# Two of the seven single tiles of the routed experts stand in a block that runs only if the routing has more than 37 groups

## The chip, the cores and the metric

The kernel runs on one core of a Trainium2 chip. The metric is the device time of one execution in microseconds (us); the time before is the median of three runs.

## What is computed

A decoder layer on 2048 rows (8 sequences of 256) of width 256, all in float32: causal self-attention with 16 heads, then three rounds of attention against a context with a gated recurrent update, then a feed-forward layer with one shared expert and eight routed ones, a layer norm after each. The change is in the routed experts:

```python
router_probs = softmax(x @ gate_w + gate_b)                    # 2048 x 8
expert_values, expert_indices = top_k(router_probs, k=2)
expert_values = expert_values / (sum(expert_values) + 1e-9)
h = gelu(einsum('bsd,edi->bsei', x, ew1) + eb1)                # 256 -> 1024, for each expert
all_outputs = einsum('bsei,eid->bsed', h, ew2) + eb2           # 1024 -> 256
moe_out = sum over the two chosen experts of value * output
x = layernorm(x + mlp(x, sh_w1, sh_b1, sh_w2, sh_b2) + moe_out)
```

Each row goes to two of eight experts, so 4096 rows are to be worked, and how many each expert gets is known only when the kernel runs.

## The kernel before

The rows are worked expert by expert, and the kernel is unrolled: the number of pieces is fixed when it is written. A group is 128 rows of one expert. A pair tile is two groups (256 rows), a single tile is one. 16 pair tiles (numbers 0 to 15, `NPAIRT`) and 7 single tiles (16 to 22, `NSINGLE`) cover any routing, since eight experts can have at most 39 groups. What a tile works on is looked up.

`place` computes for each row the line of a table `xd` in memory where its copy goes, and POOL scatters the rows there, block by block. `tables()` then counts on VectorE how many pairs and singles each expert has, and gives each tile its expert (`te`, as an integer `tei`) and the first line of its rows (`tr`, `tri`). A tile with no owner takes lines that hold zeros and the last expert, and is worked like any other. `left_no` says which left-over group a tile may take: the singles take 0 to 6, the last pair tile may take group 7.

For each tile, SP reads expert and line into registers and issues the loads: `tile_fetch` the rows `xg` (four buffers), `tile_weights` the first weight w1 (1 MB) and its bias, `tile_weights2` the second, w2 (1 MB), and its bias (two buffers each). `tile_turn` transposes the rows on TensorE, `tile_up` multiplies with w1 into PSUM `ph_t` (two buffers) and ScalarE applies the gelu into `hT_t`, `tile_down` multiplies with w2 into `pf_t`, VectorE adds the bias into `yo`, and SP stores `yo` into the table `yd`.

The order is written by hand. `TILES` lists two pairs and a single seven times, and the two last pairs behind them. The loop's turn k does the up product of tile k, issues the row fetch of k + 3 and w1 of k + 2, turns k + 1, does the down product of k - 1, and issues w2 of k + 1. The shared expert works on eight units of 256 rows (`shared_up`, `shared_down`: `ph_s`, `pf_s`): four before the tile loop, while rows are scattered and tables made, and four behind it.

Behind the loop a fixed order begins for PE, ACT, DVE and POOL (`manual_schedule`). There POOL gathers the results back from `yd`, 32 gathers of 128 rows (`fetch_back`, 16 buffers `y`), DVE weighs and adds them (`take_back`), and `finish` norms the rows and stores them, while PE works the shared units 4 to 7. The first lines of it:

```python
    shared_up(4)
    fetch_back(0)
    shared_up(5)
    fetch_back(1)
    take_back(0)
    parts(4)
    take_back(1)
```

A gather may read any line of `yd`, so it comes behind all stores of the loop.

Of the kernel before, what the change touches and what calls it, by code (L numbers as in the profile page):

```python
# [10 lines left out]
F32 = mybir.dt.float32  # L11
I32 = mybir.dt.int32
U16 = mybir.dt.uint16
AF = mybir.ActivationFunctionType
ALU = mybir.AluOpType
# [6 lines left out]
NE, FF = 8, 1024  # L22
# [11 lines left out]

RT = 256
NSTEP = NT // RT
NPAIRT = 2 * NT // RT
NSINGLE = (2 * NT + NE * (P - 1)) // P - 2 * NPAIRT  # L40
NTILE = NPAIRT + NSINGLE

TILES = [t for k in range(NSINGLE) for t in (2 * k, 2 * k + 1, NPAIRT + k)]
TILES += range(2 * NSINGLE, NPAIRT)

ROWS = NE * NT + RT

# [14 lines left out]
def decoder_kernel(  # L62
# [538 lines left out]
        count(pair_no, slice(NPAIRT + h, NTILE, 2), [[1, n]], NPAIRT)  # L601
    count(pair_row, one, [[P, NSINGLE]], NPAIRT * RT)
    nc.gpsimd.memset(left_no[:, two], float(NT))
    nc.gpsimd.memset(left_no[:, NPAIRT - 1 : NPAIRT], float(NSINGLE))
    count(left_no, one, [[1, NSINGLE]])

    gate_b = fr.tile([P, NE], F32, name="gate_b")
# [4 lines left out]
    def tt(o, a, b, op):  # L612
        nc.vector.tensor_tensor(o, a, b, op)  # L613
# [306 lines left out]
    def tables():  # L920

        pt = bank("total")[:, 0:NE]
        nc.tensor.matmul(pt, ones, before[:, nsub_all, :], start=True, stop=True)
        total = fr.tile([P, NE], F32, name="total")
        nc.vector.tensor_copy(total, pt)
        none = float(NE * NT)

        def steps_below(name, x):

            more = fr.tile([P, NE, NSTEP], F32, name=f"more_{name}")  # L930
            shape = [P, NE, NSTEP]
            tt(more, x.unsqueeze(2).to_broadcast(shape), steps_rt.unsqueeze(1).to_broadcast(shape), ALU.is_gt)
            num = fr.tile([P, NE], F32, name=f"num_{name}")
            nc.vector.tensor_reduce(num, more, AX.X, ALU.add)
            return num

        def ends(name, num):

            end = [fr.tile([P, NE], F32, name=f"end_{name}{k}") for k in range(2)]
            nc.vector.tensor_copy(end[0], num)  # L940
            q, step = 0, 1
            while step < NE:
                nc.vector.tensor_copy(end[1 - q][:, 0:step], end[q][:, 0:step])
                tt(end[1 - q][:, step:], end[q][:, step:], end[q][:, : NE - step], ALU.add)
                q, step = 1 - q, 2 * step
            return end[q]

        def owners(name, end, no):

            shape = [P, NTILE, NE]  # L950
            past = fr.tile(shape, F32, name=f"past_{name}")
            tt(past, end.unsqueeze(1).to_broadcast(shape), no.unsqueeze(2).to_broadcast(shape), ALU.is_le)
            te = fr.tile([P, NTILE], F32, name=f"te_{name}")
            nc.vector.tensor_reduce(te, past, AX.X, ALU.add)
            return te

        def looked_up(name, te, origin):
            shape = [P, NTILE, NE + 1]
            mine = fr.tile(shape, F32, name=f"mine_{name}")
            tt(mine, te.unsqueeze(2).to_broadcast(shape), experts.unsqueeze(1).to_broadcast(shape), ALU.is_equal)  # L960
            tt(mine, mine, origin.unsqueeze(1).to_broadcast(shape), ALU.mult)
            tr = fr.tile([P, NTILE], F32, name=f"tr_{name}")
            nc.vector.tensor_reduce(tr, mine, AX.X, ALU.add)
            return tr

        anyof = steps_below("any", total)
        nc.vector.tensor_scalar(total, total, -float(P), None, ALU.add)
        pairs = steps_below("pairs", total)  # L970
        left = fr.tile([P, NE], F32, name="left")
        tt(left, anyof, pairs, ALU.subtract)
        pair_end, left_end = ends("pairs", pairs), ends("left", left)

        pair_origin = fr.tile([P, NE + 1], F32, name="pair_origin")
        left_origin = fr.tile([P, NE + 1], F32, name="left_origin")
        for origin in (pair_origin, left_origin):
            nc.vector.tensor_copy(origin, first_row)
        nc.vector.scalar_tensor_tensor(
            left_origin[:, 0:NE], pairs, float(RT), first_row[:, 0:NE], ALU.mult, ALU.add  # L980
        )
        tt(pairs, pair_end, pairs, ALU.subtract)
        nc.vector.scalar_tensor_tensor(
            pair_origin[:, 0:NE], pairs, -float(RT), first_row[:, 0:NE], ALU.mult, ALU.add
        )
        te = owners("pairs", pair_end, pair_no)
        tr = looked_up("pairs", te, pair_origin)
        tt(tr, tr, pair_row, ALU.add)
        nc.vector.tensor_scalar(tr, tr, none, None, ALU.min)

        over = fr.tile([P, 1], F32, name="over")
        nc.vector.tensor_scalar(over, pair_end[:, NE - 1 : NE], -float(NPAIRT), 0.0, ALU.add, ALU.max)
        nc.vector.tensor_scalar(over, over, -2.0, None, ALU.mult)
        tt(left_no[:, one], left_no[:, one], over.to_broadcast([P, NSINGLE]), ALU.add)
        te2 = owners("left", left_end, left_no)
        tr2 = looked_up("left", te2, left_origin)
        free = fr.tile([P, NTILE], F32, name="free")
        nc.vector.tensor_scalar(free, te, float(NE), None, ALU.is_ge)
        for a, b, n in ((te, te2, float(NE)), (tr, tr2, none)):
            nc.vector.scalar_tensor_tensor(b, b, -n, free, ALU.add, ALU.mult)  # L1000
            tt(a, a, b, ALU.add)
        nc.vector.tensor_scalar(te, te, float(NE - 1), None, ALU.min)
        tei = fr.tile([P, NTILE], I32, name="tei")
        nc.vector.tensor_copy(tei, te)
        tri = fr.tile([P, NTILE], I32, name="tri")
        nc.vector.tensor_copy(tri, tr)
        return tei, tri
# [120 lines left out]
    def tile_fetch(t):  # L1128

        row = nc.sync.value_load(tri[0:1, t : t + 1], min_val=0, max_val=ROWS - RT)  # L1130
        xg = f2.tile([P, 2, D], F32, tag="xg", name=f"xg_{t}", bufs=4)[:, 0 : groups(t), :]
        load = nc.sync.dma_start(xg, rows_of(xd, row, t))
        for put in puts:
            tc.add_manual_dep(
                load.ins,
                put.ins.name,
                mybir.DependencyInfo(mybir.DependencyClass.Sync, mybir.DependencyReason.DATA),
                reason="rows of the table",
            )
        TI[t] = [row, xg]  # L1140

    def tile_weights(t):

        e = nc.sync.value_load(tei[0:1, t : t + 1], min_val=0, max_val=NE - 1)
        w1_sb = wff.tile([P, DC, FF], F32, tag="w1", name=f"w1_{t}")
        w2_sb = wff.tile([P, FC, D], F32, tag="w2", name=f"w2_{t}")
        bt = f2.tile([P, FC], F32, tag="bt", name=f"bt_{t}", bufs=3)
        b2t = f2.tile([P, D], F32, tag="b2t", name=f"b2t_{t}", bufs=3)
        nc.sync.dma_start(w1_sb, ew1[ds(e, 1), :, :].rearrange("e (c p) f -> p (e c) f", p=P))
        nc.sync.dma_start(bt, vecs[:, ds(e * FC, FC)])  # L1150
        TI[t] += [w1_sb, w2_sb, bt, b2t, e]

    def tile_weights2(t):

        row, xgT, w1_sb, w2_sb, bt, b2t, e = TI[t]
        nc.sync.dma_start(w2_sb, ew2[ds(e, 1), :, :].rearrange("e (c p) d -> p (e c) d", p=P))
        nc.sync.dma_start(b2t, b2[ds(e, 1), :].to_broadcast([P, D]))
# [12 lines left out]
    def tile_up(t):  # L1170
        row, xgT, w1_sb, w2_sb, bt, b2t, e = TI[t]
        HT["t", t] = up(w1_sb, bt, xgT, f"t{t}")

    def tile_down(t):
        row, xgT, w1_sb, w2_sb, bt, b2t, e = TI.pop(t)
        n = groups(t)
        po = down(w2_sb, HT.pop(("t", t)), f"t{t}", groups=n)
        yo = f2.tile([P, 2, D], F32, tag="yo", name=f"yo_{t}")[:, 0:n, :]
        tt(yo, po[:, 0:n, :], b2t.unsqueeze(1).to_broadcast([P, n, D]), ALU.add)
        nc.sync.dma_start(rows_of(yd, row, t), yo)  # L1180
# [68 lines left out]
    for k, t in enumerate(TILES):  # L1249
        tile_up(t)  # L1250
        for t2 in TILES[k + 3 : k + 4]:
            tile_fetch(t2)
        for t2 in TILES[k + 2 : k + 3]:
            tile_weights(t2)
        for t2 in TILES[k + 1 : k + 2]:
            tile_turn(t2)
        if k:
            tile_down(TILES[k - 1])
        for t2 in TILES[k + 1 : k + 2]:
            tile_weights2(t2)  # L1260


    tile_down(TILES[-1])
    engines = {mybir.EngineType.PE, mybir.EngineType.Activation, mybir.EngineType.DVE, mybir.EngineType.Pool}
    ctx.enter_context(tc.manual_schedule(engines=engines))
    half = NSUB // 2
# [95 lines left out]
```

## Time and profile before

| what | value |
|---|---|
| time, median of 3 runs | 1041.12 us (1041.05 to 1042.68) |
| the profiled execution's own time | 1039.3 us |
| its span, first to last instruction | 1037.6 us |
| mean granted TensorE clock | 0.999 |
| tile loop, from its first up product to the last down product on PE | 695.2 to 975.7 us |
| shared units 4 to 7 on PE behind it | 975.6 to 1031.0 us |

The profile is one execution. Engines are PE (TensorE matmul), PEld (its weight loads), DVE (VectorE), ACT (ScalarE), POOL (GpSimd) and SP, which issues the DMAs. Names such as `ph_t<-xgT,w` are out<-in by the program's tiles, L1062 is a line of the kernel. One float32 matmul of the program appears as two records, so a single tile's up product of 16 is 32 in a row. In a timeline, brackets give how long the engine was idle before, and what ended it; for a wait on several things the name can be that of one long done. Several helpers (`tt`, the norms) have one line for all their uses, so the tile's name is read with it.

### The profile page before, as it was taken

The page shows a single profiled execution, that of the slowest core. Times are in us where ns is not written, and L with a number is a line of the kernel's source. Part 1 is how long each engine was busy: PE and PEld are TensorE (multiplying, and loading weights), DVE is VectorE, ACT ScalarE, POOL GpSimd, SP SyncE. Part 2 cuts the span into 40 slices and gives each one's busy share as a digit, 9 for nine tenths or more (in the row PEclk, how much of TensorE's full clock was granted, in tenths as well). Part 3 has the DMA queues.
Part 4 walks back from the last instruction along what each step waited for, and adds up shares of the span by engine and source line. Part 5 has one row for each costly group of instructions (what it writes and reads, how often), then busy time and mean ns, then how long its engine had stood idle before and what let it go on. Part 6 is the DMA issues. An engine that isn't in the chain of part 4 may idle for free. (4 is left out here: it accounts for less than half of the span.)

```text
span 1037.6 us, 13707 instructions
## 1 busy us (share of the span) xinstructions
PE 1023.9 (99%) x4686; PEld 711.2 (69%) x4686; DVE 486.6 (47%) x1378; ACT 466.3 (45%) x1156; POOL 264.1 (25%) x280
## 2 busy tenths in 40 slices
PE   9999999999999999999999999999999999999997
PEld 5444555555546755556565567988888888888886
DVE  4778776877897542444444579600010101010157
ACT  3568776766685034455455434322222322222232
POOL 2333422633587221122212014410000000000172
PEclk9999999999999999999999999999999999999999
DMA  9844434434467399950000001166666676765143
GB/s 324 132 76 93 86 69 76 77 62 76 77 115 161 125 348 348 349 172 0 1 1 0 1 16 57 62 193 228 219 219 213 224 235 221 230 208 194 50 121 103
DMA packets 195492, 144.24 MB, mean 139 GB/s; under 512 B 107551, under 2 KB 185951, under 8 KB 195423
## 3 DMA queue, kind: packets, MB, share of 16 engines
q1 hardware_dynamic: 191263, 132.88, 45.5%
q0 software_dynamic: 3072, 8.39, 2.5%
q10 hardware_dynamic: 1088, 2.10, 0.5%
q8 instruction: 37, 0.61, 0.2%
q14 instruction: 32, 0.26, 0.1%
HBM read 72.70 MB, written 45.48 MB: 114 GB/s over the span
## 5 line engine op out<-in xcount | busy, mean ns | idle before, releaser
L1071 ACT ACTIVATE hT_t<-ph_t,bt 128x256 f32<-128x256 f32 (+1 forms) x184 | 71.3, 438 | 202.6 <-issue 139.1
L353 ACT ACTIVATE sc<-sc,nmax 128x128 f32<-128x128 f32 (+1 forms) x256 | 113.2, 443 | 86.0 <-DVE nmax L340 85.5
L368 POOL TENSOR_TENSOR sc<-sc,sums 128x256 f32<-128x256 f32 (+1 forms) x128 | 105.4, 845 | 162.8 <-DVE sums L365 162.0
L1062 PE MATMUL ph_t<-xgT,w 128*128 128x256 f32 (+1 forms) x736 | 140.3, 348 | 0.8 <-ACT hT_t L1071 0.8
L1076 PE MATMUL pf_t<-w,hT_t 128*128 128x256 f32 x624 | 138.3, 379 | 0.0
L1062 PEld LDWEIGHTS ph_t<-xgT,w 128*128 128x128 f32 x736 | 123.8, 190 | 15.0 <-ACT hT_t L1071 1.0
L756 PE MATMUL gate<-XT,whh_sb 128*128 128x512 f32 x288 | 133.8, 593 | 0.0
L1076 PEld LDWEIGHTS pf_t<-w,hT_t 128*128 128x128 f32 x624 | 116.9, 190 | 15.0
L1190 POOL DMA_INDIRECT y<-yd,slot x32 | 31.0, 969 | 308.2 <-PE ph_s L1062 298.7
L396 DVE COPY pT<-turned 128x1536 uint16<-128x1536 uint16 x64 | 89.8, 1403 | 1.2 <-DMA turned<-planes 1.2
L756 PEld LDWEIGHTS gate<-XT,whh_sb 128*128 128x128 f32 x288 | 54.2, 189 | 48.5 <-issue 46.2
L340 DVE CUSTOM_DVE_ANT_0 sc<-pp,mask 128x128 f32<-128x128 f32 (+1 forms) x256 | 75.8, 352 | 8.8 <-PE pp L328 8.2
L1167 DVE COPY xgT<-xg 128x512 f32<-128x512 f32 (+1 forms) x23 | 14.0, 610 | 131.7 <-PE xg L1165 131.7
L765 PEld LDWEIGHTS gate<-at,G 120*128 120x128 f32 x288 | 54.5, 189 | 29.9 <-issue 23.3
L613 DVE TENSOR_TENSOR yo<-pf_t,b2t 128x512 f32<-128x512 f32 (+1 forms) x23 | 14.0, 610 | 127.9 <-PE pf_t L1076 127.9
L384 ACT COPY planes<-sc 128x1536 uint16<-128x1536 uint16 x48 | 70.6, 1470 | 6.7 <-POOL sc L368 6.7
L765 PE MATMUL gate<-at,G 120*128 120x256 f32 x288 | 72.1, 379 | 0.4 <-DVE at L613 0.4
L303 PE MATMUL pq<-XT,wq_sb 128*128 128x512 f32 x128 | 63.4, 618 | 0.2 <-DVE XT L105 0.2
L303 PE MATMUL pq<-XT,wk_sb 128*128 128x512 f32 x128 | 63.2, 616 | 0.0
L313 PE MATMUL pv<-wv_sb,XT 128*128 128x512 f32 x128 | 59.7, 594 | 0.0
L410 PE MATMUL po<-pT,v 128*64 128x256 f32 (+1 forms) x512 | 55.7, 338 | 2.4 <-DVE pT L396 1.5
L426 PE MATMUL py<-wo_sb,ot 128*128 128x256 f32 x256 | 57.9, 381 | 0.0
(209 smaller groups left out, 1429.5 us busy)
## 6 DMA issues: line engine op xcount, KB each, us to landing
w<-in_ew_dram SPq DMA_DIRECT2D x46, 1024.0 KB, 5.5
xd<-zeros SPq DMA_DIRECT2D x1, 16640.0 KB, 51.3
yd<-zeros SPq DMA_DIRECT2D x1, 16640.0 KB, 99.4
xg<-xd SPq DMA_DIRECT2D x16, 256.0 KB, 5.2
yd<-yo SPq DMA_DIRECT2D x16, 256.0 KB, 5.6
b2t<-in_b_dram SPq DMA_DIRECT2D x23, 128.0 KB, 5.3
sh<-in_sh_w_dram SPq DMA_DIRECT2D x2, 1024.0 KB, 6.6
X<-in_x_dram SPq DMA_DIRECT2D x3, 512.0 KB, 11.6
```

The source lines that it names most:

```text
L303: nc.tensor.matmul(pq, w[:, dc, ts(pr, P)], XT[i][:, dc, :], start=dc == 0, stop=dc == DC - 1)
L313: nc.tensor.matmul(pv, XT[i][:, dc, ts(n, P)], wv_sb[:, dc, ts(hf, 512)], start=dc == 0, stop=dc == DC - 1)
L340: nc.vector.tensor_tensor_reduce(out=sc[:, h, seg[t]], in0=pp[h][:, seg[t]], in1=mask[:, seg[t]], scale=-(HD**-0.5), scalar=3.0e38, op0=AL ...
L353: nc.scalar.activation(sc[:, h, seg[t]], sc[:, h, seg[t]], AF.Exp, scale=-1.0, bias=nmax[:, t, h : h + 1], accum_out=sums[:, t, h : h + 1],)
L368: nc.gpsimd.tensor_tensor(sc[:, :, seg[t]], sc[:, :, seg[t]], sums[:, t, :].unsqueeze(2).to_broadcast([P, 2, w]), ALU.mult,)
L384: nc.scalar.copy(planes, words)
L396: nc.vector.tensor_copy(pT.rearrange("p h c -> p (h c)").bitcast(U16).rearrange("p (n w) -> p w n", w=2), turned.rearrange("p (w c) q -> p ...
L756: nc.tensor.matmul(pg[:, oc, :], whh_sb[:, dc, o], XT[i][:, dc, :], start=dc == 0, stop=not given and dc == DC - 1,)
L765: nc.tensor.matmul(pg[:, oc, ts(bi, S)], G[:, BPB * i + bi, o], AT_[p][:, bi, :], start=not hidden, stop=not hidden or bi == BPB - 1,)
L1062: nc.tensor.matmul(ph[:, a, 0:w], w1_sb[:, dc, ts(c, P)], rhs[:, dc, :], start=dc == 0, stop=dc == DC - 1,)
L1071: nc.scalar.activation(hT[:, c, 0:w], ph[:, a, 0:w], AF.Gelu_apprx_tanh, bias=bias[:, c : c + 1])
L1076: nc.tensor.matmul(po, hT[:, c, ts(a, P)], w2_sb[:, c, :], start=c == 0, stop=c == FC - 1)
```

## The change

Five single tiles (`NOFTEN`) stay in `TILES`. The two last (`RARE`, tiles 21 and 22) stand behind the loop in `with tc.If(first_rare < NE)`, each written out as fetch, weights, turn, up and down. The tables hand left-over groups to the five singles first, then to pair tiles that have no pair, then to the rare ones: `spare`, the number of free pair tiles, is added to the rare tiles' `left_no`, and three pair tiles instead of one may take a left-over group. One more integer in `tei` holds tile 21's expert before it is limited to 7; it is 8 (`NE`) where that tile has no owner. It is read into a register of every engine in turn k = 16 of the loop.

```diff
+NRARE = 2
+NOFTEN = NSINGLE - NRARE
-TILES = [t for k in range(NSINGLE) for t in (2 * k, 2 * k + 1, NPAIRT + k)]
-TILES += range(2 * NSINGLE, NPAIRT)
+TILES = [t for k in range(NOFTEN) for t in (2 * k, 2 * k + 1, NPAIRT + k)]
+TILES += range(2 * NOFTEN, NPAIRT)
+RARE = range(NTILE - NRARE, NTILE)
...
-    nc.gpsimd.memset(left_no[:, NPAIRT - 1 : NPAIRT], float(NSINGLE))
+    for j in range(NE - NOFTEN):
+        nc.gpsimd.memset(left_no[:, NPAIRT - 1 - j : NPAIRT - j], float(NOFTEN + j))
...
+        spare = fr.tile([P, 1], F32, name="spare")
+        nc.vector.tensor_scalar(spare, pair_end[:, NE - 1 : NE], -1.0, float(NPAIRT), ALU.mult, ALU.add)
+        nc.vector.tensor_scalar(spare, spare, 0.0, None, ALU.max)
+        rare = slice(RARE.start, NTILE)
+        tt(left_no[:, rare], left_no[:, rare], spare.to_broadcast([P, NRARE]), ALU.add)
...
+        tei = fr.tile([P, NTILE + 1], I32, name="tei")
+        nc.vector.tensor_copy(tei[:, NTILE : NTILE + 1], te[:, RARE.start : RARE.start + 1])
         nc.vector.tensor_scalar(te, te, float(NE - 1), None, ALU.min)
-        tei = fr.tile([P, NTILE], I32, name="tei")
-        nc.vector.tensor_copy(tei, te)
+        nc.vector.tensor_copy(tei[:, 0:NTILE], te)
...
         if k:
             tile_down(TILES[k - 1])
+        if k == NPAIRT:
+            first_rare = nc.values_load(tei[0:1, NTILE : NTILE + 1], min_val=0, max_val=NE)
         for t2 in TILES[k + 1 : k + 2]:
             tile_weights2(t2)


     tile_down(TILES[-1])
+    with tc.If(first_rare < NE):
+        for t in RARE:
+            tile_fetch(t)
+            tile_weights(t)
+            tile_weights2(t)
+            tile_turn(t)
+            tile_up(t)
+            tile_down(t)
```

## The prediction

> **What bounds the kernel now.** I read the page first, then the busy time of the engines by stage, then the chain of waits in order of time, then the timeline around the spot where the new block stands, and last single rows for the costs. The page and the stage row say that TensorE is full:
>
> ```profile
> PE 1023.9 (99%) x4686; PEld 711.2 (69%) x4686; DVE 486.6 (47%) x1378; ACT 466.3 (45%) x1156; POOL 264.1 (25%) x280
> PEclk9999999999999999999999999999999999999999
> ...
> 703.00:976.00 273.00, 272.43 (x1400) 242.79 (x1401) 26.70 (x45) 68.11 (x177) 0.00 (x0) 1.00 0.63 210
> ```
>
> In the third line (from 703 us, when the tile loop has just begun, to its end at 976) PE is busy for 272.43 of 273.00 us at clock 1.00, with the DMA engines at 0.63. So time taken off PE there is time taken off the end, as long as PE stays fed. The chain of waits (start, length, what) confirms it; the lines of one single tile and the end of the loop:
>
> ```profile
> 890.14 0.22 PE xg L1165 x2
> ...
> 897.27 3.71 PE ph_t L1062 x32
> ...
> 915.67 3.46 PE pf_t L1076 x16
> ...
> 961.92 13.81 PE pf_t L1076 x64
> 975.73 13.81 PE ph_s L1062 x64
> ...
> 1010.26 6.92 PE ph_s L1062 x32
> ...
> 1017.21 0.84 ACT hT_s L1071 x2
> ```
>
> The chain is PE without a break from 703.57 to 1017.19, then ACT and DVE for the last norms. A single tile stands in it three times: 2 matmuls that turn its rows (0.22), 32 of the up product (3.71), 16 of the down product (3.46).
>
> **Is the block skipped?** Everything rests on this. The reference, evaluated with its own inputs, sends 540, 521, 707, 391, 600, 463, 533 and 341 rows to the eight experts. In groups of 128 that is 5+5+6+4+5+4+5+3 = 37, in the kernel's terms 16 pairs and 5 singles. The condition needs more than 37. The nearest step to 38 is expert 7 (43 rows short of 384) or expert 4 (40 short of 640), so rounding can't reach it. With 16 pairs nothing is spare, single 5 finds no owner in either table, its expert number is 8 = NE, and `first_rare < NE` is false. Tiles 21 and 22 carry no row today either.
>
> **What is removed.** Two single tiles: 2 x (0.22 + 3.71 + 3.46) = 14.78 us of PE, all in the chain. Their 4.2 MB of weights, 16 activations, 4 vector operations and stores go too; these lie beside PE and bring nothing. The loop now ends in six pairs instead of two. A pair takes 0.44 + 6.91 + 6.91 = 14.26 us and loads about 2.4 MB with its rows and bias, 170 GB/s, under the 210 GB/s that this stage moves today, so I charge nothing; w2 is issued a whole tile ahead of its use, while
>
> ```profile
> w<-in_ew_dram SPq DMA_DIRECT2D x46, 1024.0 KB, 5.5
> ```
>
> says 5.5 us from issue to landing.
>
> **What is added to the tables.** Two scalar operations for `spare`, one add onto `left_no`, one more cast. Rows:
>
> ```profile
> L992 DVE TENSOR_SCALAR over<-end_pairs x1: 136/136/136, 670.7 to 670.7; 128x1 f32<-128x1 f32 x1
> ...
> L613 DVE TENSOR_TENSOR left_no<-left_no,over x1: 157/157/157, 671.4 to 671.4; 128x7 f32<-128x7 f32 x1
> ...
> L1004 DVE CAST tei<-te_pairs x1: 177/177/177, 674.4 to 674.4; 128x23 int32<-128x23 f32 x1
> ...
> 682.48 1.64 SPq L1132 DMA_DIRECT2D xg<-xd  x2
> ```
>
> 2 x 0.14 + 0.16 + 0.18 = 0.62 us, so `tri` is ready at 675.3 instead of 674.7. The first row fetch starts only at 682.48, because it waits for the scatters into `xd` that POOL issues until 680.8. The 0.6 us vanish in those 7 us; without that cover they would be 0.6 us. Two more POOL memsets (0.09 us each, at 330 us) lie where POOL is mostly idle: nothing.
>
> **What is added to the queues.** `values_load` puts one register load on each of five engines. SP's row is the price:
>
> ```profile
> L1130 SPq TENSOR_LOAD <-tri x23: 262/267/600, 674.8 to 723.7; - x23
> ```
>
> 0.27 us. On PE it stands ahead of `tile_weights2` in the loop's turn k = 16, long after its data; the matmuls already queued hide it, at worst 0.27 us. Behind it on ACT and DVE only work with slack is queued, POOL is idle for 299 us there, and on SP it is ahead of a w2 load with a tile of slack.
>
> **The block's edge, the unknown.** No instruction of before branches in mid-kernel, and the trace doesn't show how the semaphores that the skipped instructions would have raised are settled. What lies around it:
>
> ```profile
> 975.77 0.69 DVE L613 TENSOR_TENSOR yo<-pf_t,b2t 128x512 f32<-128x512 f32 x1 [6.22 <-PE pf_t L1076]
> ...
> 979.47 0.98 POOL L1190 DMA_INDIRECT y<-yd,slot  x1 [298.71 <-PE ph_s L1062]
> ...
> 1012.11 0.84 ACT L1071 ACTIVATE hT_s<-ph_s,vec_sb 128x256 f32<-128x256 f32 x2
> ...
> L1358 SPq DRAIN  x3: 7/13/130, 1036.7 to 1037.3; - x3
> ...
> L1358 PEldq EVENT_SEMAPHORE  x2: 51/51/51, 1036.9 to 1037.6; - x2
> ```
>
> Today PE runs from `pf_t` into `ph_s` without a gap, and under those shared matmuls the last `yo` is written, stored, and gathered back (gather 3.9 us after PE's tail began). The bounds: from below 0.3 us (a register test and a branch; a gain is excluded, as PE has no gap to close). From above, PE waits for everything that the arm could touch, the last store into `yd` among it: it stands until the first gather could start, 3.9 us. The nearest row is the end of the program, where all engines meet: drains and semaphore passes from 1036.7 to 1037.6, 0.9 us a meeting. One to enter and one to leave make 1.8 us, with nothing of it hidden since PE has no work on the other side of the edge. I take 1.8 and keep 0.3 and 3.9 as ends. The gather may also come later than 3.9 us after the tail's start, since POOL must pass the edge too. Its slack is small: take-back of block 1 waited for gathers at 1001.76, the norms behind it hold ACT until the 1012.11 row, and PE would have missed that buffer at about 1013.5, 0.5 us after ACT freed it at 1012.95. In the case taken PE is late by as much as POOL, so nothing is added.
>
> Two rules of the Trainium skill speak against the change. "TensorE: Matmul & The Clock Gate" (Part 1, the HAM clock gate) says that PE falls to half clock after an idle window of about 3.4 us and needs another 3.4 us of work to come back. The row above has PEclk 9 in every slice, and PE's longest stop in the tile stage is 0.83 us, so no run shows it here. With my 1.8 us nothing follows; with the upper end of 3.9 us the rule adds an estimated 3.4 / 2 = 1.7, making 5.6. "Runtime: NRT & Kernel Launch" (Instruction fetch mechanics) says that a taken branch to a target outside the resident pages stalls until the page is fetched. The row:
>
> ```profile
> q8 instruction: 37, 0.61, 0.2%
> ```
>
> 37 packets of 0.61 MB in all, 16.5 KB each; if q8 is PE's, 9,372 instructions make 253 per packet. The skipped arm has 2 x 50 matmuls and as many weight loads on PE, 200, less than one packet. So the next page should hold the target: 0 in my sum. By the rule's other case it would be one transfer, 2.1 us (the fastest store into `yd`) to 5.5 (a weight load).
>
> **Sum.** On the profiled execution: span 1037.6 - 14.78 + 1.8 = 1024.6. That execution took 1039.3 in all, 1.8 less than the median 1041.12; carried over, 1041.1 - 14.8 + 1.8 = 1028.1.
>
> **Rivals.**
> *The edge waits for the store.* For it: the arm writes `yd` and reuses the `yo` buffers, so what guards the arm may wait for that store. Against: PE's own part of the arm touches neither. Cost 3.9 to 5.6 us, in all 1030.2 to 1032.0; with the table or gather a little late, 1032.5.
> *Code is fetched after the branch.* For it: five instruction streams jump at once, and SP's or ACT's may sit near a page's end. Against: PE's arm is short. 1.8 to 5.6 plus 2.1 to 5.5: 1030.2 to 1037.4.
> *Slower: the block runs.* If the switch is true for this routing (a slip in the tables or in the order of clip and copy), both tiles run alone at the edge: nothing prefetched, so PE stands for about 7.9 us (median landing of the first weights), and the 4.2 MB at about 230 GB/s last until 18 us; then the second down product 3.5, `yo` 0.4, the store and restart 3.9: 26 us in place of 14.8, and 1.8 for the edges. 1041.1 + 13 = 1054. It decides when the eighth expert number is below 8; by my count it is 8. The same sign needs over 14.8 us of edge otherwise, nearly four whole store waits in a row.
>
> **How the numbers follow.** Forecast 0.55 (1026.6 to 1029.5, from the edge's 0.3 to 3); store wait 0.25; code fetch 0.10; block runs 0.03; an edge dearer than all of this 0.05, of which half ends near today's time; more gain than 14.8 us 0.02. The range 1026.0 to 1034.5 holds the first two and most of the third. A difference below 0.2% (2.1 us, about the spread of the runs before) can't be told from none. Faster 0.91, same 0.03, slower 0.06.
>
> **What would show it.** Right: PE's count of `pf_t` falls by 32, to 592, and of `ph_t` by 64, to 672; the last `pf_t` ends near 961; a hole on PE of 1 to 3 us stands before `ph_s`; first gather 3 to 5 us behind the last `pf_t`. A hole near 4 us with a clock below 1 behind it means the store rival; a hole longer than that, with instruction packets in it, the code rival; 736 matmuls of `ph_t` mean that the block ran. I am wrong if PE shows new gaps inside the loop, or if the tail from `ph_s` to the end grows.

## The result, and the profile after

The changed kernel takes 1026.46 us (median of 4 runs, 1024.52 to 1028.01) against 1041.9 (1041.05 to 1042.8): ratio 0.9857, 95% interval 0.9843 to 0.9872, so 13 to 16 us less. The profiled execution took 1024.52 us with a span of 1022.8, where that of before took 1039.3 with 1037.6. A second set of runs gave 0.9851 (0.983 to 0.987).

The page of the changed kernel, with the busy row of the engines, the clock row and the two groups of the tile loop on PE:

```profile
PE 1009.1 (99%) x4586; PEld 697.2 (68%) x4586; DVE 485.0 (47%) x1378; ACT 461.0 (45%) x1140; POOL 263.6 (26%) x282
...
PEclk9999999999999999999999999999999999999999
...
L1075 PE MATMUL ph_t<-xgT,w 128*128 128x256 f32 (+1 forms) x672 | 132.5, 355 | 0.8 <-ACT hT_t L1084 0.8
...
L1089 PE MATMUL pf_t<-w,hT_t 128*128 128x256 f32 x592 | 131.1, 379 | 0.0
```

PE has 100 matmuls fewer, two single tiles of 50 each: 64 of `ph_t` (736 before), 32 of `pf_t` (624), 4 that turn rows. PE's busy time fell by 14.8 us and the span by 14.8. PEclk reads 9 in every slice, as before.

The timeline of the changed kernel at the spot of the block (start, length, engine, line; in brackets the idle time before):

```profile
946.89 13.98 PE L1089 MATMUL pf_t<-w,hT_t 128*128 128x256 f32 x64
...
954.72 7.30 SPq L1193 DMA_DIRECT2D yd<-yo  x2
960.91 0.69 DVE L618 TENSOR_TENSOR yo<-pf_t,b2t 128x512 f32<-128x512 f32 x1 [6.21 <-PE pf_t L1089]
960.99 13.68 PEld L1075 LDWEIGHTS ph_s<-XT,sh 128*128 128x128 f32 x64 [0.52 <-issue]
961.02 14.05 PE L1075 MATMUL ph_s<-XT,sh 128*128 128x256 f32 x64
963.08 0.84 ACT L1084 ACTIVATE hT_s<-ph_s,vec_sb 128x256 f32<-128x256 f32 x2 [15.15 <-PE ph_s L1075]
964.58 0.98 POOL L1203 DMA_INDIRECT y<-yd,slot  x1 [283.93 <-ACT hT_s L1084]
```

The same spot in the kernel before:

```profile
961.75 13.98 PE L1076 MATMUL pf_t<-w,hT_t 128*128 128x256 f32 x64
...
975.57 13.98 PE L1062 MATMUL ph_s<-XT,sh 128*128 128x256 f32 x64
```

There the `pf_t` row ends at 961.75 + 13.98 = 975.73 and the next begins at 975.57: in a stream without a gap the next row begins 0.16 us before the end of the one ahead of it. In the changed kernel the last `pf_t` row ends at 946.89 + 13.98 = 960.87, so the next would begin at 960.71. It begins at 961.02, and PE lost 961.02 - 960.71 = 0.31 us at the block's edge. I call this the hole. The first gather comes 3.87 us behind 960.71; before it was 3.9 behind 975.57.

The accounts of the two traces close. The tile loop begins at 695.13 instead of 695.23. From there to `ph_s` it takes 265.89 us instead of 280.34, which is 14.45 less: 14.78 of two tiles and the hole back. From `ph_s` to the end it is 61.78 instead of 62.03. Together 0.10 + 14.45 + 0.25 = 14.8.

What each engine did at the edge is in the rows of the block's line. "q" stands for an engine's queue; the columns are shortest, median and longest duration in ns, then first and last start:

```profile
L1279 SPq EVENT_SEMAPHORE  x9: 17/17/17, 962.3 to 963.7; - x9
L1279 POOLq COMPARE_BRANCH  x1: 45/45/45, 675.4 to 675.4; - x1
L1279 ACTq COMPARE_BRANCH  x1: 45/45/45, 947.1 to 947.1; - x1
L1279 ACTq EVENT_SEMAPHORE  x1: 17/17/17, 948.0 to 948.0; - x1
L1279 PEldq COMPARE_BRANCH  x1: 358/358/358, 956.8 to 956.8; - x1
L1279 PEldq EVENT_SEMAPHORE  x1: 51/51/51, 960.9 to 960.9; - x1
L1279 DVEq COMPARE_BRANCH  x1: 72/72/72, 961.7 to 961.7; - x1
L1279 DVEq EVENT_SEMAPHORE  x1: 21/21/21, 961.9 to 961.9; - x1
L1279 SPq COMPARE_BRANCH  x1: 53/53/53, 962.1 to 962.1; - x1
```

The engines do not meet. POOL branches at 675.4, over 270 us ahead of the others, ACT at 947.1 as soon as its last gelus are issued, PE at 956.8 while its last matmuls still run. Each engine that skips work raises a semaphore here once its own earlier work is done: PE at 960.9, when the last `pf_t` ends, VectorE at 961.9, behind its last `yo`. SP raises nine from 962.3 to 963.7 (seven in the run with one rare tile); which is for what the trace doesn't say. POOL skips nothing and raises none. PE is at work again at 961.02, before VectorE and SP raise theirs, so it waits for neither. What it pays is its own drain: the next matmul starts only when the last one has ended, where before the two overlapped.

### The profile page after: what moved, and what is told of

Read it like the earlier page. It is cut to its first block, busy times and chain, and to the rows that moved or that the text cites. A ratio compares the mean times of both kernels' runs of the same rounds, so it can differ in the third digit from the quotient of the medians.

```text
span 1022.8 us, 13461 instructions
## 1 busy us (share of the span) xinstructions
PE 1009.1 (99%) x4586; PEld 697.2 (68%) x4586; DVE 485.0 (47%) x1378; ACT 461.0 (45%) x1140; POOL 263.6 (26%) x282
## 5 line engine op out<-in xcount | busy, mean ns | idle before, releaser
L1084 ACT ACTIVATE hT_t<-ph_t,bt 128x256 f32<-128x256 f32 (+1 forms) x168 | 66.1, 444 | 193.0 <-issue 122.9
L1075 PE MATMUL ph_t<-xgT,w 128*128 128x256 f32 (+1 forms) x672 | 132.5, 355 | 0.8 <-ACT hT_t L1084 0.8
L1089 PE MATMUL pf_t<-w,hT_t 128*128 128x256 f32 x592 | 131.1, 379 | 0.0
L1075 PEld LDWEIGHTS ph_t<-xgT,w 128*128 128x128 f32 x672 | 116.2, 190 | 14.8 <-ACT hT_t L1084 1.0
L1089 PEld LDWEIGHTS pf_t<-w,hT_t 128*128 128x128 f32 x592 | 111.0, 190 | 14.3
```

The source lines that it names most:

```text
L1075: nc.tensor.matmul(ph[:, a, 0:w], w1_sb[:, dc, ts(c, P)], rhs[:, dc, :], start=dc == 0, stop=dc == DC - 1,)
L1084: nc.scalar.activation(hT[:, c, 0:w], ph[:, a, 0:w], AF.Gelu_apprx_tanh, bias=bias[:, c : c + 1])
L1089: nc.tensor.matmul(po, hT[:, c, ts(a, P)], w2_sb[:, c, :], start=c == 0, stop=c == FC - 1)
```

## Experiments

All compare with the kernel before on the same chip. The first four ran on a chip where before took 1071.3 us and the next six where it took 1040.9, so ratios are compared across, not times. The traces from the first chip hold stretches that the others lack: PE stands for 6.5 to 7.2 us once, near 680 us, and in the shared units behind the tile loop it runs single matmuls with 0.8 to 2.2 us between them for some 15 us, with the clock at 0.50. Their cause isn't shown. None of them lies between `pf_t` and `ph_s`, where the clock is 1.00 in these traces but for the run whose block ran, so the holes read there stand; the times carry these stretches with them.

**The block taken out.** The two tiles and the block are both gone, so it serves only routings of up to 37 groups.

```diff
-        if k == NPAIRT:
-            first_rare = nc.values_load(tei[0:1, NTILE : NTILE + 1], min_val=0, max_val=NE)
...
-    with tc.If(first_rare < NE):
-        for t in RARE:
...
```

> The changed kernel without the block and without the register loads: the two tiles are gone altogether. Theory (the gain is two single tiles of PE time, the edge is nearly free): PE passes from the last pf_t to ph_s without the 0.3 us hole, the span is 0.3 us under the changed kernel's, so about 1022.5, and the time about 1026, 15.1 us under before. Rival (the edge costs 1.8 us as the forecast had it, and something else gave 1.5 back): 1.5 to 2 us under the changed kernel, about 1024.5.

Measured: ratio 0.9853 (0.982 to 0.988), the change's 0.9857. The timing alone can't separate 0.3 from 1.8 us. Its timeline can; the end of `pf_t` and the start of `ph_s`:

```profile
974.83 1.67 PE L1089 MATMUL pf_t<-w,hT_t 128*128 128x256 f32 x7
...
976.34 6.21 PE L1075 MATMUL ph_s<-XT,sh 128*128 128x256 f32 x28
```

974.83 + 1.67 = 976.50, so the next row begins 0.16 us before this one ends: no hole. The change's 0.31 us is therefore the block's.

**The block alone.** All seven single tiles stay in the loop; what the change adds is added.

```diff
-TILES = [t for k in range(NOFTEN) for t in (2 * k, 2 * k + 1, NPAIRT + k)]
-TILES += range(2 * NOFTEN, NPAIRT)
+TILES = [t for k in range(NSINGLE) for t in (2 * k, 2 * k + 1, NPAIRT + k)]
+TILES += range(2 * NSINGLE, NPAIRT)
```

> All seven single tiles stay in the loop, and the block that never runs stands behind it as well, with its tables and register loads: only what the change adds. Theory: before plus 0.3 us of PE hole, 1042.2, not to be told from before. Rival (edge 1.8): 1043.7, and a PE hole near 2 us behind the last pf_t.

Measured: ratio 1.0013 (0.9998 to 1.0028), which is -0.2 to +2.9 us on 1041.9 and holds both. The trace:

```profile
978.67 13.98 PE L1089 MATMUL pf_t<-w,hT_t 128*128 128x256 f32 x64
...
992.79 10.38 PE L1075 MATMUL ph_s<-XT,sh 128*128 128x256 f32 x47
```

Without a gap `ph_s` would begin at 978.67 + 13.98 - 0.16 = 992.49; it begins at 992.79, a hole of 0.30 us again. The theory stands by the hole; the time doesn't decide.

**One rare tile.** `NRARE = 1`.

> One single tile in the block instead of two. Theory: half of the tiles' 14.78 us, less the same edge: before - 7.39 + 0.3 = 1034.8, PE hole 0.3 us. Rival (a fixed gain from other things, such as the three pair tiles that may take a single group): not half, 1028 to 1032.

Measured: ratio 0.9930 (0.991 to 0.995). On 1041.9 that is 7.3 us less (4.9 to 9.6), where the theory has 7.1 and the rival 10 to 14, and the hole is 0.31 us again (981.77 to 982.08). The gain goes with the number of tiles.

**The block runs.**

```diff
-    with tc.If(first_rare < NE):
+    with tc.If(first_rare < NE + 1):
```

> The condition is made true for this routing (< NE + 1), so the block runs with its two empty tiles. It prices the taken side. The rival of the prediction that ended slower put 26 us on the edge plus 1.8: 1054. Theory with the edge at 0.3: 1041.9 - 14.8 + 26 + 0.3 = 1053.4. Rival: the loads of both tiles overlap better than I worked out (tile 21's weights are there after 5.5 us, and the second's while the first is worked): 1041.9 - 14.8 + 5.5 + 14.8 + 4 = 1051 or less.

Measured: ratio 1.0101 (1.0070 to 1.0132), slower than before by 7 to 14 us; on 1041.9 the middle is 1052.4, and the interval, 1049 to 1056, holds both numbers of the expectation. From the end of `pf_t` (975.99) to `ph_s` (1002.64) PE's work is held up for 26.65 us, where the prediction's slower rival had 26 plus 1.8. The parts came out otherwise, as the timeline of this run shows:

```profile
980.28 0.66 PE L1178 MATMUL xg<-ident,xg 128*128 128x128 f32 x2 [4.12 <-DMA xg<-xd]
...
984.35 6.72 PE L1075 MATMUL ph_t<-xgT,w 128*128 128x128 f32 x32 [3.41 <-DMA w<-in_ew_dram]
...
990.90 3.62 PE L1089 MATMUL pf_t<-w,hT_t 128*128 128x256 f32 x16
995.37 3.98 PE L1075 MATMUL ph_t<-xgT,w 128*128 128x128 f32 x32 [0.63 <-DVE xgT L1180]
...
999.18 3.62 PE L1089 MATMUL pf_t<-w,hT_t 128*128 128x256 f32 x16
```

The first weights came 5.1 us after their issue at 979.25, not 7.9, and the second tile's came wholly under the first tile's work: its up product waited for DVE alone, 0.63 us. So the loads were cheaper than I had them. The first up product, though, took 6.55 us to the next row's start where a single tile's takes 3.71, and the second took 3.81. Busy time and granted clock (the third number from the right) in three stretches tell why:

```profile
980.28:984.35 4.07, 0.66 (x2) 0.29 (x3) 0.42 (x1) 0.00 (x0) 0.00 (x0) 0.50 0.94 313
984.35:987.85 3.50, 3.50 (x16) 3.50 (x17) 0.00 (x0) 0.63 (x2) 0.00 (x0) 0.50 0.78 266
995.37:999.20 3.83, 3.83 (x33) 3.77 (x34) 0.00 (x0) 1.88 (x6) 0.00 (x0) 1.00 0.20 68
```

Behind a stop of 4.12 us and another of 3.41, PE ran at clock 0.50, and the up product lost 2.8 us.

**PE held at the edge, first try.** PE was to wait for 2 or 12 vector copies behind the block. This is the edit for 2; for 12, `range(11)` stands in place of `range(1)`. The second theory of the clock in these expectations is the idle window of about 3.4 us for which the prediction names its page.

```diff
+    chain = [f1.tile([P, BLK], F32, name=f"chain{j}") for j in range(2)]
+    nc.vector.tensor_copy(chain[0], Z[3][:, 0:2, :].rearrange("p a b -> p (a b)"))
+    for j in range(1):
+        nc.vector.tensor_copy(chain[1 - j % 2], chain[j % 2])
+    pt = bank("held")[:, 0:P]
+    nc.tensor.transpose(pt, chain[1][:, 0:P], ident)
     shared_up(4)
+    nc.vector.tensor_copy(chain[0][:, 0:P], pt)
     fetch_back(0)
```

> The changed kernel, and behind the block PE waits for a chain of 2 vector copies (128x512) before ph_s: the wait that the prediction's first rival had, made short. A copy should take 0.35 to 0.69 us, the chain begins with the last yo 0.9 us behind PE's end, so PE stands 1.6 to 2.3 us. Both theories of the clock (a stop costs only its length; a stop of over about 3.4 us also halves the clock for a while) expect the changed kernel plus the hole, + 1.3 to 2 us, at clock 1.0.

> The same with 12 copies: a hole of 5.1 to 9.2 us. Theory (a stop costs only its length): the changed kernel plus the hole less 0.3. Rival (the clock falls as well, as after the stops in the run whose block ran): the first ph_s matmuls take near twice 0.22 us each for up to 3.4 us, and the time is about 1.7 us more than the hole.

Measured: ratios 0.9867 and 0.9866 (0.985 to 0.989 both). With 2 copies or 12, PE stood equally long, so the copies did not hold it. The run with 12:

```profile
L1293 DVE COPY chain<-chain x11: 395/417/420, 653.4 to 658.6; 128x512 f32<-128x512 f32 x11
...
L1295 PE MATMUL held<-ident,chain x1: 300/300/300, 965.4 to 965.4; 128*128 128x128 f32 x1
```

The copies were made at 653 us: they depended on nothing in the block, and in the program as scheduled they stand in front of it. The runs don't test what they were meant to. What they do show is the price of meeting one engine: the wait that was left is for DVE to pass its own edge, behind the last `yo`. The timeline of the run with 2 copies:

```profile
965.63 0.30 PE L1295 MATMUL held<-ident,chain 128*128 128x128 f32 x1 [1.23 <-DVEq L1279]
```

PE stood for 1.23 us there. Its clock, the third number from the right, stayed at 1.00 behind it:

```profile
965.60:966.60 1.00, 0.97 (x5) 0.92 (x6) 0.29 (x1) 0.00 (x0) 0.00 (x0) 1.00 0.54 195
```

In times this is about 1.6 us over the change itself, with intervals that overlap.

**Two blocks, and the change once more.**

```diff
-    with tc.If(first_rare < NE):
-        for t in RARE:
+    for t in RARE:
+        with tc.If(first_rare < NE):
```

> Each of the two rare tiles in a block of its own, with the same condition: two edges one behind the other, nothing run. Theory (an engine passes an edge once its own earlier work is done, with no meeting of engines): the PE hole grows from 0.3 to 0.6 us at most, less if the second check waits for nothing, and the time can't be told from the changed kernel. Rival (an edge costs a meeting of all engines): the hole grows by 0.9 us or more.

> The changed kernel itself, beside the three others on the same chip. Theory: before less 14.5 us (two single tiles, less a hole of 0.3 us). Rival (the measured 15.4 us hold something else beside the tiles): 15.4 or more.

Measured: two blocks 0.9859 (0.984 to 0.988), the change 0.9851 (0.983 to 0.987). The timeline with two blocks, and what PE's queue did at its two edges:

```profile
960.93 1.46 PE L1089 MATMUL pf_t<-w,hT_t 128*128 128x256 f32 x6
...
962.97 11.46 PE L1075 MATMUL ph_s<-XT,sh 128*128 128x256 f32 x52 [0.58 <-PEq L1280]
```

```profile
L1280 PEldq COMPARE_BRANCH  x2: 219/288/358, 958.4 to 962.6; - x2
L1280 PEldq EVENT_SEMAPHORE  x2: 51/51/51, 962.4 to 962.9; - x2
```

Without a gap `ph_s` would begin at 960.93 + 1.46 - 0.16 = 962.23; it begins at 962.97, a hole of 0.74 us. That is over the 0.6 that the theory allowed and under the rival's 1.2 (0.3 and 0.9 more). The rows show what the theory left out: the first branch runs at 958.4 under queued matmuls, but the second comes at 962.6, behind the first block's semaphore and so behind the drain. Its 0.22 us lies bare, and with its semaphore the second edge costs 0.43. For the repeat, the middle of 15.5 us lies at the rival's number, its interval (13.5 to 17.6) holds 14.5. Whether something beside the tiles gives up to a microsecond can't be told from these times; the traces' account above leaves 0.35 us outside the loop.

**PE held at the edge, second try.** The chain now begins with the last `yo`, so it can't be early.

```diff
+        return yo
...
-    tile_down(TILES[-1])
+    last_yo = tile_down(TILES[-1])
+    chain = [f1.tile([P, BLK], F32, name=f"chain{j}") for j in range(2)]
+    nc.vector.tensor_copy(chain[0], last_yo.rearrange("p a b -> p (a b)"))
+    for j in range(1):
+        nc.vector.tensor_copy(chain[1 - j % 2], chain[j % 2])
...
+    pt = bank("held")[:, 0:P]
+    nc.tensor.transpose(pt, chain[1][:, 0:P], ident)
     shared_up(4)
+    nc.vector.tensor_copy(chain[0][:, 0:P], pt)
```

> The copies of the two hold runs had been made early, so PE met only VectorE at the edge there. Now the chain begins with a copy of the last yo, so it can't be early: 2 copies of 0.42 us. PE stands about 0.2 + 0.7 + 0.84 + 0.2 = 1.9 us. Both theories of the clock: the changed kernel + 1.6 us, clock 1.0.

> The same with 12 copies: PE stands about 0.9 + 12 x 0.42 + 0.7 = 6.6 us. Theory (a stop costs only its length): the changed kernel + 6.3, about 1032.5. Rival (after so long a stop the clock is at half for a while, as in the run whose block ran, where an up product took 6.55 us for 3.71 behind a stop of 3.41): clock 0.50 in the first 3 us of ph_s and 1.7 us more, the changed kernel + 8.

Measured: ratios 0.9904 (0.989 to 0.992) and 0.9950 (0.993 to 0.997), which is 5.5 and 10.3 us over the change's 0.9851 (in the traces, from the end of `pf_t` to the end of `ph_s`, 18.48 and 23.53 us against 14.20, so 4.3 and 9.3 more, inside the intervals). The run with 2 copies, timeline and then five stretches of a microsecond:

```profile
963.50 0.30 PE L1296 MATMUL held<-ident,chain 128*128 128x128 f32 x1 [2.67 <-DVEq L1284]
963.64 15.67 PE L1075 MATMUL ph_s<-XT,sh 128*128 128x256 f32 x64
```

```profile
963.50:964.50 1.00, 1.00 (x5) 0.90 (x6) 0.29 (x1) 0.00 (x0) 0.00 (x0) 0.99 0.00 0
964.50:965.50 1.00, 1.00 (x4) 0.80 (x3) 0.00 (x0) 0.00 (x0) 0.96 (x1) 0.50 0.00 0
965.50:966.50 1.00, 1.00 (x4) 0.82 (x3) 0.00 (x0) 0.00 (x0) 0.70 (x2) 0.50 0.24 61
966.50:967.50 1.00, 1.00 (x3) 0.74 (x3) 0.19 (x1) 0.84 (x2) 0.70 (x2) 0.50 0.18 70
967.50:968.50 1.00, 1.00 (x5) 0.87 (x4) 0.30 (x1) 0.00 (x0) 0.70 (x2) 0.80 0.42 131
```

PE stood for 2.67 us, ran one more microsecond at full clock, then some 3.4 us at half, and the 64 matmuls of `ph_s` took 15.67 us instead of 14.05: 1.62 us on top of the stop. Both theories had clock 1.00 here and both are wrong on this run. With 12 copies the same work took 15.91 us behind a stop of 7.38, 1.86 on top, as the rival with the clock had it:

```profile
969.79 0.44 PE L1296 MATMUL held<-ident,chain 128*128 128x128 f32 x1 [7.38 <-DVE chain L1283]
970.03 15.91 PE L1075 MATMUL ph_s<-XT,sh 128*128 128x256 f32 x64
```

The stops are each some 0.8 us longer than I had worked out, because VectorE must pass its own edge as well (with 12 copies it is idle for 0.70 us between the sixth copy and the seventh, where its register load and its branch lie).

## Why the prediction was right

It had 1028.1 us, range 1026.0 to 1034.5, faster at 0.91. The measured median is 1026.46. The mechanism held; one term of the sum was mis-sized, and one term was right for another reason than the one given. The median lies only 0.5 us above the low end of the range: what held it is the 0.3 us that the prediction kept as an end of its bracket and did not take. Its own sign for the edge, a hole of 1 to 3 us, did not come.

- *The block is skipped.* Right: the branch rows stand alone, and `ph_t` and `pf_t` count 672 and 592, as predicted.
- *14.78 us of PE.* Right: 14.45 in the loop and 0.31 lost at the edge make 14.76. The run with one tile gave half, the run without a block no more than the hole.
- *The loop stays fed.* Right: PE is busy for 85.80 of 85.80 us from 875 to 960.8, the six last pairs.
- *The tables are covered.* Right: the first row fetch is at 682.37 (682.48 before).
- *The register loads are hidden.* Right in effect, mis-sized in length: 0.48 us on PE (at 893.6, under matmuls) and 0.47 to 0.74 on the others, where SP's row gave 0.27. Not all came in turn k = 16: those of SP and POOL ran at 674.6, ahead of the first row fetch, and VectorE's only at 961.1, just ahead of its branch; nobody waited for VectorE there.
- *The edge, 1.8 us.* This is the failed term: it is 0.31. The prediction took as its nearest row the end of the program, where all engines meet, and counted two meetings of 0.9 us. (Even that price was read loosely: PE's row there holds two semaphores, at 1036.9 and 1037.6, so the 0.9 us may hold both meetings.) A skipped block is no meeting: each engine closes its own account and goes on. The low end of the bracket, 0.3 us, was the value. PE's branch, 4 us early under queued matmuls, adds nothing; the drain behind the last matmul is all. The two-block run shows the price of a branch without that lead. What a meeting would have cost was measured too, with VectorE alone 1.23 us of idle.
- *The store rival.* It didn't come: SP ended the issue of the last store at 954.72 + 7.30 = 962.02, when PE had been at work again for 1.0 us, so PE can't have waited for it. The half clock that the Trainium skill ("TensorE: Matmul & The Clock Gate", Part 1, the HAM clock gate) gave as a further price is real here: 1.62 and 1.86 us measured, behind stops of 2.67 and 7.38 us, where 1.7 was estimated from that page.
- *The code rival.* A fetch came, but no stall. PE's branch runs at 956.8, and from 957.8 to 958.9 all DMA queues together moved one packet, of instructions:

```profile
q8 instruction: 1, 0.02, 5.6%
```

It begins 1.1 us behind the branch. That holds for all eight skipping branches that took PE 0.36 us, in eight traces; no packet follows within 9 us the two that took 0.22 and 0.23 us (the second of two blocks, and the one-tile run). That the packet is fetched for the branch is inferred from this. It takes 0.9 to 1.4 us, so it has landed 2.5 us behind the branch at the latest, while the matmuls queued ahead run for 4.1. The prediction's 0 for this term held, but hardly for its reason, that the next page holds the target: PE branched early enough to cover a fetch. That was luck.

- *The slower rival.* The switch is false, so it didn't come; made true, it costs 26.65 us against 27.8 worked out, by a sum whose parts differed: loads cheaper, clock dearer.

The 1.5 us between the prediction and the sum with the edge as measured are the edge. The median's last few tenths are scatter: the runs of the changed kernel lie up to 3.5 us apart, and a part of that is the clock, as the last section shows. A slip in the chances moves nothing: an edge of 3 us gives 1029.3 by the prediction's own sum, where it has 1029.5.

## What to carry to other kernels

Work that is laid out for the worst case and is seldom needed can stand in a conditional block when the engine that bounds the stage pays only its own drain there: read what each engine waits for at the edge, not that there is an edge. Let that engine reach its branch while earlier work is still queued: then the branch and a fetch of code behind it cost nothing, and one block is cheaper than two (0.31 against 0.74 us). Count on the data deciding: by the run whose block ran, a routing of 38 or 39 groups makes this kernel some 10 us slower than before, so the gain is worth the share of routings that skip. And price a wait on TensorE by the clock behind it too: a stop of 2.7 us cost 1.6 more.

## What the runs showed of the hardware

- A skipped block costs an engine one compare-and-branch (45 ns on ACT and POOL, 50 to 53 on SP, 56 to 72 on DVE, 219 to 358 on PE's queue) and, where it has work in the block, a semaphore raise (SP seven to nine); PE's hole was 0.30 to 0.31 us in three kernels and 0.74 with two blocks.
- The TensorE clock fell to 0.50 behind stops of 2.67, 4.12 and 7.38 us and not behind one of 1.23, nor behind one of 1.61 in the run without a block:

```profile
633.69 1.99 PE L1075 MATMUL ph_s<-XT,sh 128*128 128x256 f32 x8 [1.61 <-ACT z L807]
...
631.00:640.00 9.00, 7.23 (x35) 5.78 (x35) 8.32 (x27) 6.76 (x14) 0.00 (x0) 1.00 0.00 0
```

After the stop of 2.67 it fell only when PE had been at work again for 1.0 us, 3.7 us after the stop began. The skill's page named above puts it at an idle window of about 3.4 us, with a window that runs free of the program. The stop of 2.67 is shorter, so here the measurement decides: a stop under 3 us can already cost the clock.

- The clock can also fall where PE does not stop, and in one execution of a kernel and not in another. Near 650 us PE runs 32 matmuls of 128x8, then 32 of `ph_s`, with no idle time between. Three microseconds of those `ph_s`, in the first profile of the changed kernel and in that of its repeat:

```profile
653.00:656.00 3.00, 3.00 (x15) 2.66 (x14) 2.96 (x30) 2.47 (x5) 0.00 (x0) 1.00 0.00 0
653.00:656.00 3.00, 3.00 (x8) 2.36 (x7) 3.00 (x31) 2.06 (x3) 0.00 (x0) 0.50 0.00 0
```

The 32 of `ph_s` take 7.15 us in the one and 8.84 in the other, so this alone moves a run by 1.7 us. The program is the same, so its order of work alone doesn't decide whether the clock falls. Whether a stop between 1.61 and 2.67 us can cost the clock, and whether the small matmuls are what made it fall here, stays open.
